# The router's scores in a cross-attention and mixture-of-experts kernel: weights stationary, four token tiles in four column groups, and a turn back

## The chip, the cores and the metric

The kernel runs on one core of one Trainium2 chip. A core has engines that work side by side, each through its own list of instructions in order: TensorE (PE in the profile; PEld is its loading of the stationary operand), VectorE (DVE), ScalarE (ACT), GpSimd (POOL) and SyncE (SP, which here only issues DMAs). The metric is the device time of one execution in microseconds; lower is better. Before the change the median of three runs is 830.52 us (829.87 to 831.75).

## The reference

One transformer layer with 4 x 1024 = 4096 tokens of width 256, all in fp32:

```python
x = x + xattn(_layernorm(x), ctx, ctx, Wq, ..., gamma, beta)   # 16 heads, 77 context rows
x = x + ffn(_layernorm(x), Wg, W1, W2, W3, Ws1, Ws2, Ws3)
# in ffn
scores = jax.nn.softmax(xf @ Wg, axis=-1)          # Wg is 256 x 32: 32 experts
weights, indices = jax.lax.top_k(scores, TOP_K)    # TOP_K = 4
# each expert e: swiglu of the tokens that chose it, times their weight, added to y
z = swiglu(xf, Ws1, Ws2, Ws3)                      # shared expert
return (y + z).reshape(B, S, D)
```

The change touches the one product `xf @ Wg`, the router's scores: 4096 tokens x 256 by 256 x 32.

## The kernel before

The 4096 tokens are 8 blocks of 512, and a block is 4 tiles of 128 (`NB`, `NC`). After a preparation stage that folds the projections of keys and values into two products per batch (`headed`, `products`; lines 237 and 262), one loop runs over the 32 tiles t. At each t it does the attention of tile t (`scores` in three groups of heads, `soften`, `divide`), turns and multiplies the probabilities of tile t-1 (`turn_p`, `output`, `residual`), and does a piece of the work for three blocks at different stages: the block ahead is normalised and turned, the block behind (`ffn`) is settled, and the block two behind (`old`) goes through the router. Everything in the loop stands in `as_written()`, which ties each engine to the order in which the code issues its instructions. So the code's order is the order on every engine.

The router of block `old` is spread over a block's four tiles: with c = t mod 4, c = 0 turns the normalised block (`turn_ffn`, result `xnT`, features on partitions), c = 1 computes the scores (`gate`), shifts them by their maximum and takes the exponential (`chances`) and picks the four best (`choose`), c = 2 marks them (`mark`), c = 3 counts and places them (`count`, `place`), and POOL then scatters the rows into DRAM (`send`, line 672). Blocks 0 to 5 go through `gate` inside the loop, at t = 9, 13, 17, 21, 25 and 29. Block y = 6 has it after the loop, and block z = 7 in the stage behind that, where the tables for the experts are made (`tables`) and the shared expert runs for y and z (`shared_in`, `shared_mid`, `shared_out`). Then come 160 expert tiles (lines 1059 to 1093) and the final gather.

`gate` makes one PSUM bank `lg` per block: for each tile c and each half k of the features, a 128 x 128 piece of `xnT` is the stationary operand and 32 columns of `wg` stream past it, so that tokens come out on partitions and experts on columns:

```python
nc.tensor.matmul(lg[:, c * NE : (c + 1) * NE],
                 xnT[:, k, c * P : (c + 1) * P], wg[:, k, :], start=(k == 0), stop=(k == KC - 1))
```

Each fp32 matmul of the code appears as two LDWEIGHTS and two MATMUL instructions in the profile; a transpose appears as one of each. DVE then reads `lg` twice (maximum at line 574, difference at line 576), and ACT takes the exponential (line 577). PSUM has 8 banks, handed out in turn by `bank`.

Of the kernel before, what the change touches and what calls it, by code (L numbers as in the profile page):

```python
# [9 lines left out]
F32 = mybir.dt.float32  # L10
I32 = mybir.dt.int32
U32 = mybir.dt.uint32
AF = mybir.ActivationFunctionType
# [3 lines left out]
P = 128  # L17
NE = 32
# [12 lines left out]
def kernel(  # L31
# [23 lines left out]
    nc = tc.nc  # L55
# [5 lines left out]
    KC = D // P  # L61
    TB = 512
    NB = T // TB
    NC = TB // P
# [22 lines left out]
    def bank(name):  # L87
        return ps.tile([P, 512], F32, tag="bank", name=name)


    ident = const.tile([P, P], F32, name="ident")
# [56 lines left out]
    sm = ctx.enter_context(tc.tile_pool(name="sm", bufs=4, side="right"))  # L148
# [5 lines left out]
    wg = late.tile([P, KC, NE], F32, name="wg")  # L154
# [255 lines left out]
    def bias_in(blk):  # L410
        nc.gpsimd.memset(qTs[blk][0:1, 0, :], 1.0)  # L411

    def scores(t, g):

        b, blk, o = t * P // (T // B), t // NC, t % NC * P
        h0, h1 = GROUPS[g]
        if g == 0:
            p = wkp.tile([P, NH, SK], F32, tag="p", name=f"p_{t}")
            su = sm.tile([P, NH], F32, tag="su", name=f"su_{t}", bufs=2)
            mx = sm.tile([P, NH], F32, tag="mx", name=f"mx_{t}", bufs=2)  # L420
            probs[t], sums[t] = p, (su, mx)
        su, mx = sums[t]
        sc = bank(f"sc_{t}_{g}")
        for k in range(KC):
            nc.tensor.matmul(  # L425
                sc[:, : (h1 - h0) * SK],
                qTs[blk][:, k, o : o + P],
                mq[:, b, k, h0 * SK : h1 * SK],
                start=(k == 0),
                stop=(k == KC - 1),  # L430
            )
        sv = sc[:, : (h1 - h0) * SK].rearrange("p (h s) -> p h s", s=SK)
        nc.vector.tensor_reduce(mx[:, h0:h1], sv, AX.X, ALU.max, negate=True)  # L433
        return sv

    def soften(t, g, sv):

        h0, h1 = GROUPS[g]
        su, mx = sums[t]
        for h in range(h0, h1):  # L440
            nc.scalar.activation(  # L441
                probs[t][:, h, :],
                sv[:, h - h0, :],
                AF.Exp,
                bias=mx[:, h : h + 1],
                accum_out=su[:, h : h + 1],
            )
# [105 lines left out]
        xnTs[blk] = xnT  # L553

    def gate(blk):
        xnT = xnTs.pop(blk)
        lg = bank(f"lg_{blk}")
        for c in range(NC):
            for k in range(KC):
                nc.tensor.matmul(  # L560
                    lg[:, c * NE : (c + 1) * NE],
                    xnT[:, k, c * P : (c + 1) * P],
                    wg[:, k, :],
                    start=(k == 0),
                    stop=(k == KC - 1),
                )
        lgs[blk] = lg

    def chances(blk):

        lg = lgs.pop(blk)
        lv = lg[:, : NC * NE].rearrange("p (c e) -> p c e", e=NE)
        mx = sm.tile([P, NC], F32, tag="rmx", name=f"rmx_{blk}", bufs=2)
        nc.vector.tensor_reduce(mx, lv, AX.X, ALU.max)
        pr = sm.tile([P, NC, NE], F32, tag="pr", name=f"pr_{blk}", bufs=2)
        nc.vector.tensor_tensor(pr, lv, mx.unsqueeze(2).to_broadcast([P, NC, NE]), ALU.subtract)
        nc.scalar.activation(pr, pr, AF.Exp)
        lgs[blk] = pr

    def choose(blk):  # L580

# [169 lines left out]
    with as_written():  # L751
        for t in range(NT):
            blk, c = t // NC, t % NC
            ffn, old = blk - 1, blk - 2
            ahead = blk + 1 < NB
            if c == 0 and blk + 2 < NB:
                xts[blk + 2] = load(blk + 2)
            if t == 0:

                nc.sync.dma_start(xr[NE * PLACES :, :], none)  # L760
                nc.sync.dma_start(
                    xr[: NE * PLACES, :].rearrange("(e q) r -> q e r", q=PLACES)[:P],
                    none.unsqueeze(1).to_broadcast([P, NE, ROW]),
                )
            if t == 18:
                nc.sync.dma_start(ws13[:, :, 0, :], Ws1.rearrange("(k p) f -> p k f", p=P))
                nc.sync.dma_start(ws13[:, :, 1, :], Ws3.rearrange("(k p) f -> p k f", p=P))
                nc.sync.dma_start(ws2, Ws2.rearrange("(k p) f -> p k f", p=P))
            if t in parts:
                load_experts(*parts[t])  # L770
            if c == 1 and ahead:
                scale_in(blk + 1)
            if c == 1 and ffn >= 0:
                measure_out(ffn, 2, 4)
            if c == 3 and ahead:
                bias_in(blk + 1)
            if c == 3:
                measure_out(blk, 0, 2)
            if c == 3 and ffn >= 0:
                measure_ffn(ffn)  # L780
            if c == 1 and old >= 0:
                gate(old)
                chances(old)
            if c == 3 and old >= 0:
                count(old)
            sv = [scores(t, g) for g in range(2)]
            soften(t, 0, sv[0])
            soften(t, 1, sv[1])
            sv.append(scores(t, 2))
            if t >= 1:  # L790
                for i in range(3):
                    turn_p(t - 1, i)
            soften(t, 2, sv[2])
            if c == 0 and old >= 0:
                turn_ffn(old)
            if c == 2 and ahead:
                turn_in(blk + 1)
            if c == 0 and ahead:
                measure_in(blk + 1)
            if c == 1 and old >= 0:  # L800
                choose(old)
            if c == 2 and old >= 0:
                mark(old)
            if c == 3 and old >= 0:
                place(old)
            invert(t)
            divide(t)
            if c == 1 and ahead:
                norm_in(blk + 1)
            if c == 3 and ffn >= 0:  # L810
                norm_ffn(ffn)
            if c == 3:
                settle(blk, 0)
            elif ffn >= 0:
                settle(ffn, c + 1)
            if c >= 2 and ahead:
                keep(blk + 1, 2 * c - 4, 2 * c - 2)
            if t >= 11:
                b11, c11 = divmod(t - 11, NC)
                send(b11, c11 * TOPK, (c11 + 1) * TOPK)  # L820
            if t >= 1:
                residual(t - 1, output(t - 1))


        z, y = NB - 1, NB - 2
        assert BA == y
        msum_a = sm.tile([P, NE], F32, tag="msum_a", name="msum_a", bufs=1)
        nc.vector.tensor_copy(msum_a, msum)
        left = [(y - 1, i) for i in range(NK)]

        def sends(n):
            for blk, i in left[:n]:
                send(blk, i, i + 1)
            del left[:n]

        del left[:4]
        measure_out(z, 2, 3)
        settle(z, 1)
        sends(3)
        turn_ffn(y)  # L840
        for i in range(3):
            turn_p(NT - 1, i)
        settle(z, 2)
        residual(NT - 1, output(NT - 1))
        measure_out(z, 3, 4)
        gate(y)
        chances(y)
        settle(z, 3)
        sends(2)
        measure_ffn(z)  # L850
# [85 lines left out]
    with as_written():  # L936
        for part in range(5):
            load_experts(*parts[NT + 1 + part])
        ta = tables("a", msum_a, NA)
        choose(y)  # L940
        shared_in(y, 0, AF.Tanh)
        norm_ffn(z)
        mark(y)
        sends(7)
        shared_mid(y, 0)
        next(ta)
        shared_in(y, 1, AF.Tanh)
        turn_ffn(z)
        count(y)
        gate(z)  # L950
        next(ta)
        place(y)
        assert not left
        left += [(y, i) for i in range(NK)]
        chances(z)
        next(ta)
        shared_mid(y, 1)
        shared_out(y)
        next(ta)
        choose(z)  # L960
        shared_in(z, 0, AF.Silu)
        mark(z)
        count(z)
        msum_z = sm.tile([P, NE], F32, tag="msum_z", name="msum_z", bufs=1)
        nc.vector.tensor_copy(msum_z, msum)
        tz = tables("z", msum_z, NJ - NA)
        sends(5)
        shared_mid(z, 0)
        place(z)
        left += [(z, i) for i in range(NK)]  # L970
        shared_in(z, 1, AF.Silu)
        shared_add(y)
        shared_mid(z, 1)
        sends(11)
        shared_out(z)
        shared_add(z)
# [261 lines left out]
```

## Time and profile before

| What | Value |
|---|---|
| Median of the timed runs | 830.52 us |
| The profiled execution: its own time | 791.69 us |
| Its span, first to last instruction | 789.9 us |
| Granted TensorE clock over the span | 0.989 |
| POOL busy | 442.3 us (56%) |
| ACT busy | 338.9 us (43%) |
| `gate` on PE (line 560) | 128 MATMULs, 14.9 us busy |
| Share of the chain that ended last: PE | 70% |
| Share of that chain: DVE, ACT, DMA, POOL | 11%, 6%, 6%, 4% |

The profiled execution is 39 us shorter than the median of the timed runs. Stages and waits are read from the profiled one; times of the two kinds are not mixed.

In the profile a line such as `L560 PE MATMUL lg<-wg,xnT 128*128 128x32` reads: line 560, TensorE, matmul that writes `lg` from `wg` and `xnT`; 128*128 is the part of the array in use (rows by columns), and 128x32 the streamed operand. The chain of waits is followed back from the last instruction, at each step to what released it. A matmul's duration includes its way through the array; what the next one has to wait for is the distance from start to start, which is shorter.

### The profile page before, as it was taken

Reading aid. Unit: us, or ns where it says so; the run is one execution under the profiler, and the core shown is the slowest. Engines: PE = TensorE matmul, PEld = TensorE weight load, DVE = VectorE, ACT = ScalarE, POOL = GpSimd, SP = SyncE. Lnnn points to the kernel's source line nnn. Section 1 sums busy time; section 2 is a strip of 40 time slices with the busy share of each in tenths; the row PEclk is TensorE's granted clock in tenths of the full one; section 3 lists DMA queues with packets and bytes.
Section 4 is the critical chain, followed back from the end, with each engine's and each line's share of the span. In section 5 each row is a group of like instructions: output and inputs, shape, how many; then the busy total and the mean of one; then the engine's idle time right before and its main releaser. Section 6 shows DMA issues by size and latency. Waiting matters only on the chain.

```text
span 789.9 us, 13517 instructions
## 1 busy us (share of the span) xinstructions
PE 756.0 (96%) x3690; PEld 574.9 (73%) x3690; DVE 546.1 (69%) x1499; ACT 338.9 (43%) x1610; POOL 442.3 (56%) x520
## 2 busy tenths in 40 slices
PE   6999999999999999999997899999999999999996
PEld 4775777777777777777774578888888888885544
DVE  1774465777777767775766676666777777775995
ACT  0647666666776567666542122222222222221110
POOL 2003333445778777677687667776555655553441
PEclk9899999999999999999998999999999999999998
DMA  9930000302317131513127646675646464626993
GB/s 288 331 93 1 1 0 2 109 25 73 107 58 236 51 116 58 163 57 110 52 94 228 198 145 195 214 228 196 184 150 187 145 193 139 195 87 245 386 404 141
DMA packets 81928, 116.21 MB, mean 147 GB/s; under 512 B 10507, under 2 KB 66239, under 8 KB 81855
## 3 DMA queue, kind: packets, MB, share of 16 engines
q1 hardware_dynamic: 61823, 68.37, 27.9%
q0 software_dynamic: 13824, 38.82, 13.5%
q10 hardware_dynamic: 6208, 8.17, 2.9%
q8 instruction: 31, 0.51, 0.3%
q14 instruction: 42, 0.34, 0.2%
HBM read 64.59 MB, written 50.73 MB: 146 GB/s over the span
## 4 chain that ended last, share of the span: by engine, by line
PE 70%; DVE 11%; ACT 6%; DMA 6%; POOL 4%; issue 3%; ACTq 0%; DVEq 0%; POOLq 0%; SPq 0%
PE peh L1067 17%; PE po L492 14%; PE sc L425 12%; PE py L1088 8%; ACT p L441 5%; PE pgT L1059 4%; DMA gy<-ys 3%; POOL xr L672 2%; PE phT L1081 2%; PE pz L728 2%; PE pvo L262 2%; PE pp L474 2%; DVE y L1146 1%; DVE mx L433 1%; PE lg L560 1%
## 5 line engine op out<-in xcount | busy, mean ns | idle before, releaser
L1093 POOL DMA_INDIRECT ys<-y,place x160 | 153.5, 959 | 90.3 <-DVE y L1092 52.0
L441 ACT ACTIVATE p<-sc,mx 128x77 f32<-128x77 f32 x512 | 159.0, 351 | 90.1 <-DVE mx L433 90.1
L1067 PE MATMUL peh<-we,gT 128*128 x640 | 164.8, 380 | 2.0 <-DVE gT L1061 1.3
L492 PE MATMUL po<-we,pT 128*128 128x256 f32 (+1 forms) x640 | 146.3, 383 | 4.6 <-DVE pT L479 4.3
L456 POOL TENSOR_TENSOR p<-p,su 128x385 f32<-128x385 f32 (+1 forms) x96 | 90.9, 972 | 105.2 <-DVE su L451 77.4
L672 POOL DMA_INDIRECT xr<-xn,row x128 | 127.8, 998 | 35.6 <-issue 33.7
L425 PE MATMUL sc<-we,qT 128*128 128x385 f32 (+1 forms) x384 | 138.1, 509 | 0.9 <-POOL qT L411 0.9
L492 PEld LDWEIGHTS po<-we,pT 128*128 128x128 f32 (+1 forms) x640 | 118.4, 190 | 25.9 <-DVE pT L479 7.9
L1075 ACT ACTIVATE h<-peh 128x128 f32<-128x128 f32 x160 | 44.3, 277 | 199.6 <-PE peh L1067 199.6
L441 ACT ACTIVATION_READ_ACCUMULATOR p<-sc,mx 128x1 f32 x512 | 119.2, 233 | 0.0
L1067 PEld LDWEIGHTS peh<-we,gT 128*128 128x128 f32 x640 | 109.2, 190 | 10.7 <-DVE gT L1061 1.5
L425 PEld LDWEIGHTS sc<-we,qT 128*128 128x128 f32 x384 | 71.6, 189 | 53.6 <-issue 25.4
L1076 DVE TENSOR_TENSOR h<-peh,h 128x128 f32<-128x128 f32 x160 | 46.5, 291 | 74.4 <-ACT h L1075 73.2
L1088 PE MATMUL py<-we,ehT 128*128 x320 | 95.6, 381 | 0.0
L433 DVE TENSOR_REDUCE mx<-sc 128x5 f32<-128x385 f32 (+1 forms) x96 | 54.7, 580 | 44.0 <-PE sc L425 43.7
L1092 DVE TENSOR_SCALAR y<-py,own 128x256 f32<-128x256 f32 x160 | 77.4, 484 | 0.9 <-PE py L1088 0.6
L1061 DVE COPY gT<-pgT 128x256 f32<-128x256 f32 x160 | 66.3, 414 | 0.0
L1059 PE MATMUL pgT<-ident,g 128*128 128x128 f32 x320 | 61.1, 273 | 0.0
L1088 PEld LDWEIGHTS py<-we,ehT 128*128 128x128 f32 x320 | 48.3, 191 | 12.2 <-ACT ehT L1083 0.3
L1059 PEld LDWEIGHTS pgT<-ident,g 128*128 128x128 f32 x320 | 44.7, 141 | 16.0 <-PE phT L1081 0.3
L728 PE MATMUL pz<-ws,hT 128*128 128x256 f32 x128 | 34.3, 419 | 11.7 <-DVE hT L717 6.9
L474 PEld LDWEIGHTS pp<-ident,p 128*128 128x128 f32 x320 | 36.1, 139 | 11.4 <-issue 5.5
(200 smaller groups left out, 997.3 us busy)
## 6 DMA issues: line engine op xcount, KB each, us to landing
g<-xr SPq DMA_DIRECT2D x160, 136.0 KB, 3.1
gy<-ys SPq DMA_DIRECT2D x16, 1024.0 KB, 7.9
xr<-y SPq DMA_DIRECT2D x1, 4352.0 KB
y<-in_x SPq DMA_DIRECT2D x8, 512.0 KB, 5.1
out<-y ACTq DMA_DIRECT2D x16, 256.0 KB, 5.4
xnd<-xnT SPq DMA_DIRECT2D x6, 512.0 KB
we<-in_W SPq DMA_DIRECT2D x8, 384.0 KB, 5.3
ys<-y,place POOLq DMA_INDIRECT x160, 2.5
```

The lines of the kernel that those rows point to most:

```text
L425: nc.tensor.matmul(sc[:, : (h1 - h0) * SK], qTs[blk][:, k, o : o + P], mq[:, b, k, h0 * SK : h1 * SK], start=(k == 0), stop=(k == KC - 1),)
L433: nc.vector.tensor_reduce(mx[:, h0:h1], sv, AX.X, ALU.max, negate=True)
L441: nc.scalar.activation(probs[t][:, h, :], sv[:, h - h0, :], AF.Exp, bias=mx[:, h : h + 1], accum_out=su[:, h : h + 1],)
L456: nc.gpsimd.tensor_tensor(p[:, h0:h1, :], p[:, h0:h1, :], su[:, h0:h1].unsqueeze(2).to_broadcast([P, h1 - h0, SK]), ALU.mult,)
L492: nc.tensor.matmul(po[:, :D], pT[:n, i, :], vo[b][:n, i, :], start=(i == 0), stop=(i == KT - 1))
L672: sct = nc.gpsimd.indirect_dma_start(out=xr, out_offset=bass.IndirectOffsetOnAxis(ap=row[:, i : i + 1], axis=0), in_=xn[:, c, :], in_offse ...
L1059: nc.tensor.transpose(pt[:, k * P : (k + 1) * P], g[:, j % RG, k * P : (k + 1) * P], ident)
L1061: nc.vector.tensor_copy(gT.rearrange("p k t -> p (k t)"), pt[:, :D])
L1067: nc.tensor.matmul(ph[:, : 2 * H], gT[:, k, :], we[:, ds(ev[j] * EW + k * 2 * H, 2 * H)], start=(k == 0), stop=(k == KC - 1),)
L1088: nc.tensor.matmul(py[:, :D], hT, we[:, ds(ev[j] * EW + KC * 2 * H, D)], start=True, stop=True)
L1092: nc.vector.tensor_scalar(y, py[:, :D], own[:, i, 1:2], None, ALU.mult)
L1093: sent = nc.gpsimd.indirect_dma_start(out=ys, out_offset=bass.IndirectOffsetOnAxis(ap=place_[:, i : i + 1], axis=0), in_=y, in_offset=None,)
```

## The change

`gate` swaps the operands. The weights `wg[:, k, :]`, 128 x 32, are stationary, and a 128 x 128 piece of `xnT` streams. The result of tile c has experts on partitions and tokens on columns, and lands on partitions 32c to 32c + 31 of the bank; `tile_position=(0, c * NE)` places it in columns 32c to 32c + 31 of the array. The loop order is turned: k outside, c inside. So `lg[:, :128]` holds four groups of 32 experts below one another.

A new `turn_gate` brings it back: ACT copies `lg[:, :128]` into the tile `pr`, TensorE transposes it as one 128 x 128 piece into a new bank `lt`. `chances` reads `lt` in place of `lg`, and its exponential is moved into a function of its own, `powers`. In the loop `gate` stays ahead of the first two `scores`; `turn_gate` and `chances` come behind them, and `powers` comes behind the first `soften`. In the two later places `turn_gate` stands just ahead of `chances` and `powers` just behind it.

```diff
     def gate(blk):
         xnT = xnTs.pop(blk)
         lg = bank(f"lg_{blk}")
-        for c in range(NC):
-            for k in range(KC):
+        for k in range(KC):
+            for c in range(NC):
                 nc.tensor.matmul(
-                    lg[:, c * NE : (c + 1) * NE],
+                    lg[c * NE : (c + 1) * NE, :P],
+                    wg[:, k, :],
                     xnT[:, k, c * P : (c + 1) * P],
-                    wg[:, k, :],
                     start=(k == 0),
                     stop=(k == KC - 1),
+                    tile_position=(0, c * NE),
                 )
         lgs[blk] = lg
+    def turn_gate(blk):
+        pr = sm.tile([P, NC, NE], F32, tag="pr", name=f"pr_{blk}", bufs=2)
+        flat = pr.rearrange("p c e -> p (c e)")
+        nc.scalar.copy(flat, lgs.pop(blk)[:, :P])
+        lt = bank(f"lt_{blk}")
+        nc.tensor.transpose(lt[:, :P], flat, ident)
+        lgs[blk] = lt, pr
     def chances(blk):
-        lg = lgs.pop(blk)
-        lv = lg[:, : NC * NE].rearrange("p (c e) -> p c e", e=NE)
+        lt, pr = lgs.pop(blk)
+        lv = lt[:, : NC * NE].rearrange("p (c e) -> p c e", e=NE)
...
-        pr = sm.tile([P, NC, NE], F32, tag="pr", name=f"pr_{blk}", bufs=2)
         nc.vector.tensor_tensor(pr, lv, mx.unsqueeze(2).to_broadcast([P, NC, NE]), ALU.subtract)
-        nc.scalar.activation(pr, pr, AF.Exp)
         lgs[blk] = pr
+    def powers(blk):
+        nc.scalar.activation(lgs[blk], lgs[blk], AF.Exp)
...
             if c == 1 and old >= 0:
                 gate(old)
-                chances(old)
             if c == 3 and old >= 0:
                 count(old)
             sv = [scores(t, g) for g in range(2)]
+            if c == 1 and old >= 0:
+                turn_gate(old)
+                chances(old)
             soften(t, 0, sv[0])
+            if c == 1 and old >= 0:
+                powers(old)
             soften(t, 1, sv[1])
...
         gate(y)
+        turn_gate(y)
         chances(y)
+        powers(y)
...
+        turn_gate(z)
         chances(z)
+        powers(z)
```

## The prediction

> **What bounds the kernel now.** I read the table of stretches first, for the stages in which the router runs. Its columns are the stretch, its length, then PE, PEld, DVE, ACT and POOL busy, clock, DMA share and GB/s.
>
> ```profile
> 150.00:380.00 230.00, 228.27 (x1107) 173.67 (x1107) 170.28 (x463) 153.22 (x802) 160.07 (x198) 1.00 0.32 101
> 400.00:430.00 30.00, 23.17 (x120) 16.27 (x118) 21.16 (x74) 10.14 (x20) 24.25 (x30) 0.95 0.58 181
> 450.00:700.00 250.00, 248.31 (x1372) 208.71 (x1373) 176.93 (x585) 65.75 (x303) 160.62 (x168) 1.00 0.55 177
> ```
>
> In the loop (150 to 380 us) PE is busy 99% of the time; every other engine has a quarter or more to spare. Between loop and experts (400 to 430) it is not: PE idles 7 of 30 us. The experts are again 99% PE. So time saved on PE in the loop should reach the end, and time saved between the stages only where PE or its successor ends the wait.
>
> Next the chain of waits around one gate (start, duration, what), here t = 13:
>
> ```profile
> 189.59 4.32 PE po L492 x20
> 193.92 1.71 PE lg L560 x16
> 195.62 4.23 PE sc L425 x12
> ```
>
> PE goes from `output` through the gate into `scores` without a gap: the gate is 1.71 us of PE, 16 steps of 107 ns, though only 32 columns stream in each. The rows of the tile `lg` say what paces it: loads of 128 columns at 192 ns each, overlapping their neighbours.
>
> ```profile
> L560 PEld LDWEIGHTS lg<-wg,xnT x128: 188/192/192, 149.8 to 424.0; 128*128 128x128 f32 x128
> L560 PE MATMUL lg<-wg,xnT x128: 193/276/277, 150.0 to 424.0; 128*128 128x32 f32 x128
> ```
>
> **The new gate on PE.** It removes 16 wide loads with 32-column streams and adds 16 narrow loads (32 columns) with 128-column streams. One such stream costs 109 ns: `turn_ffn`'s transposes (line 547) are 8 of 128 columns in 0.87 us. One after the other, 16 would take 1.74 us, as much as now. All depends on whether the four column groups run side by side. No row has column groups, but the preparation has row groups: `products` alternates between two halves of 64 rows. The chain shows it beside `headed`, same 308 columns, whole array:
>
> ```profile
> 43.44 8.30 PE pkT L237 x32
> 51.74 8.49 PE pm L262 x64
> ```
>
> `headed` takes 259 ns an instruction, `products` 133 ns: the two row groups overlap fully, and this with fp32 and its two instructions to a matmul. If column groups do as well, the 16 fall into 4 rounds of 4: 4 x 0.109 + 0.02 for starting offsets = 0.46 us. I take this value, as the nearest row. The bounds are 0.46 (all four overlap), 0.98 (only neighbours overlap: 9 steps of 0.109) and 1.74 (none).
>
> **The change of array shape.** The Trainium skill speaks against the change here: "TensorEngine Tiling (Array Packing)", Key Properties, says that changing the tiling mode drains TensorE. The trace has such a change in the table step, which uses a 32 x 32 corner between whole-array matmuls:
>
> ```profile
> 424.04 0.28 PE L560 MATMUL lg<-wg,xnT 128*128 128x32 f32 x1
> 424.25 0.22 PE L891 MATMUL p_end_a<-nt_a,tri_in 32*32 32x1 f32 x2
> 424.39 0.70 PE L728 MATMUL pz<-ws,hT 128*128 128x256 f32 x2
> ```
>
> The last `lg` would hand over at 424.04 + 0.11 = 424.15; `p_end` starts at 424.25, so going in costs 0.10. It then takes 0.14 for two one-column matmuls of some 0.05 each: 0.04 on the way out. And the first two `pz` end after 0.70, where the usual step of 0.216 (`po`: 4.32 / 20) plus 0.38 gives 0.60: another 0.10 for a load that is no longer hidden. Together 0.25 us per round trip. Were the drain free, each gate would gain 0.25 more.
>
> The same skill, "TensorE: Matmul & The Clock Gate", Part 3, What overlaps and what doesn't, says that a load overlaps running matmuls only where the row group differs, and that matmuls run strictly in order. Column groups share all their rows, so by the rule the loads would lie bare: a quarter of the 107 ns of a wide one, 27 ns each (an estimate), 0.43 us per gate, and strict order with two instructions to a matmul would allow neighbours alone to overlap. By the rule the gate is 0.98 + 0.43 = 1.41 us, by the rows 0.46. The `lg` rows contradict the first half: loads of 192 ns start every 107 ns on the same 128 rows, beside matmuls of 276 ns. The `pm` row contradicts the second: neighbours alone would also give 133 ns there, but the trace starts two of them together at the very first (eight instructions span 1.31 us from 51.67 on: 0.10 for a bare load, 3 more pair steps of 0.26 and a 0.42 end, so the pairs fill from the start). I follow the rows.
>
> **The turn back on PE.** One transpose, 0.11 us (0.87 / 8). In the loop it stands behind the first two `scores`, 2.9 us after the gate; the copy that it needs is done long before.
>
> Sum per gate in the loop: 0.10 + 0.46 + 0.15 + 0.11 = 0.82 against 1.71, a gain of 0.89 us. Six such gates: **5.3 us**.
>
> **ACT and DVE in the loop.** ACT gets a copy of 128 x 128 (0.31 us, as the exponential of the same shape). It falls into time in which ACT waits anyway:
>
> ```profile
> L577 ACT ACTIVATE pr<-pr 128x128 f32<-128x128 f32 x8 | 2.5, 309 | 30.5 <-DVE pr L576 30.5
> ```
>
> Eight exponentials had 30.5 us of idle time before them, 2.94 at t = 13. The exponential itself moves out of that idle time into the softmax stream, where 11 heads of 0.30 follow. It delays ACT by 0.31, and by nothing for its input: `pr` should be ready about 0.1 us before `soften` 0 ends (the second maximum ends 0.85 after its scores, then two DVE steps of 0.3). Behind it queue `soften` 1, ACT's copies of `pT`, and for those PE waits in `output`. At t = 13 ACT's copy ends at 201.98 and the ninth `po`, its first reader, starts at 202.92: 0.94 us of cover. Without it each gate would pay 0.3. On DVE the two small steps (0.26 and 0.29) move behind two maxima, into the 0.73 us for which DVE waits for the third group of scores. The extra bank per gate shifts the rotation by one; each bank it meets had its last reader over 1 us earlier. POOL's `divide` of t-1 ends at 196.0, PE's `turn_p` starts at 199.7 and would at 198.8: still covered. I cost these at nothing.
>
> **Block y, after the loop.** Here `turn_gate` follows at once, so PE waits for the copy: gate 410.08 to 410.64 (0.10 + 0.46), 0.17 until the result is out, copy 0.31 plus handover 0.09, bare load 0.10, transpose 0.11: the shared expert starts at 411.4 where it started at 411.79. That gains nothing, because PE then waits for ACT's normalised block:
>
> ```profile
> 419.74 0.33 PE L547 MATMUL pxn<-ident,xn 128*128 128x128 f32 x1 [0.16 <-ACT xn L362]
> 420.24 0.33 PE L547 MATMUL pxn<-ident,xn 128*128 128x128 f32 x1 [0.16 <-ACT xn L362]
> 420.73 0.44 PE L547 MATMUL pxn<-ident,xn 128*128 128x128 f32 x2 [0.16 <-ACT xn L362]
> ```
>
> These waits come from POOL's sends and its pow (line 347), which the gate does not touch. They also swallow a late start: with no overlap the shared expert would start 0.9 late, and the fourth transpose still come on time. Zero.
>
> **Block z.** PE goes from the gate (422.45) to `p_end`, and DVE waits for it:
>
> ```profile
> 424.50 0.15 DVE L893 COPY end_a<-p_end_a 32x1 f32<-32x1 f32 x1 [1.46 <-PE p_end_a L891]
> 429.86 0.80 PE L728 MATMUL pz<-ws,hT 128*128 128x256 f32 x1 [4.76 <-DVE hT L720]
> ```
>
> From there DVE is busy without a gap until `hT` at 429.8, for which PE waits 4.76 us. So `p_end` decides. It comes 1.80 after the gate's start; it will come 0.10 + 0.46 + 0.10 = 0.66 after it, 1.14 us earlier, less than DVE's idle 1.46. POOL's sends end that wait nowhere. Copy and transpose fall into PE's idle 4.76. Gain **1.1 us**; what is late next is DVE's own chain, unchanged.
>
> **Sum:** 5.3 + 1.1 = 6.4 us off the profiled 791.69. The runs shown have a median 39 us above that execution; I take the gain over in microseconds (stretched alike it would be 6.7): 830.52 - 6.4 = **824.1 us**.
>
> **The rivals.**
>
> *Only neighbours overlap* (0.98 per gate): gains 0.37 x 6 + 0.6 = 2.8 us, **827.7**. For it: that rule of strict order; against it: the first pair of `pm`.
>
> *Column groups take turns, slower than before.* The place is line 560. Row groups read different rows, while four column groups each stream all 128 rows of different data; no row shows that this can be fed side by side. Against it: the same Part 3 gives a measured 2.38 times for three column tiles, from which I estimate 1.74 x 3 / (4 x 2.38) = 0.55 for the gate, near my 0.46; no row here shows it. Price per gate: 0.10 + 1.74 + 0.15 + 0.11 = 2.10, a loss of 0.39, six times 2.4, and 0.1 at block z: **833.0**. It decides from the point at which 16 streams take over 1.35 us (1.71 less 0.36), 84 ns a step. With bare loads in addition (0.43 x 7) it would be 836.
>
> *The PE gain is eaten by ACT* since copy and exponential cost 0.62 per gate: only where the cover of 0.94 is gone. All six would then lose up to 0.3 each: 825.9, inside the range.
>
> **How the numbers follow.** Full overlap 0.54, neighbours 0.21, taking turns 0.20, other losses 0.05. Likeliest: 824.1, by itself 822.5 to 826.5. The range 822.5 to 833.0 takes in the neighbours and most of turn-taking. A difference of 0.2% (1.7 us) is about what a measurement of this kernel can tell from none. Faster by more: all of the first, nearly all of the second: 0.72. Slower by more: most of the third, part of the others: 0.18. Within: 0.10.
>
> **What would show it.** In the changed profile: line 560's loads with 128*32 and its starts in groups of four; chain pieces from `po` to `sc` of 0.7 us instead of 1.71; `lt` without a wait in the loop; `pT` ready before the ninth `po`; PE's wait for `hT` unchanged at block z. Wrong if those starts stand 0.1 us apart, or if the first `sc` behind a gate starts over 1.3 us after the gate.

## The result, and the profile after

| | Median | Lowest to highest | Runs |
|---|---|---|---|
| Kernel before | 831.01 us | 829.87 to 831.75 us | 4 |
| Changed kernel | 825.71 us | 824.51 to 826.42 us | 4 |

The ratio is 0.9934, with a 95% interval of 0.9918 to 0.995. By the medians it is 5.3 us faster, by the interval 4.2 to 6.8, where 6.4 had been forecast.

One thing has to be known before the profiles are compared. The kernel before takes about 790 us on some chips and about 830 us on others: 789.87, 789.95 and 790.81 us beside three groups of the experiments below, 831.01 and 830.33 us beside the first comparison and one later run. By its length, its profile came from a chip of the first kind, the changed kernel's from one of the second. So the two are compared only in the loop and in the stage just behind it. For what comes later, a profile of the changed kernel from a chip of the first kind (e5_after_again) is used.

The gate on the chain of waits of the changed kernel, at the same t = 13 as in the prediction (start us, us, what):

```profile
188.67 4.34 PE po L492 x20
193.01 0.57 PE lg L561 x16
193.59 3.04 PE sc L425 x8
196.63 0.11 PE lt L576
196.74 1.29 PE sc L425 x4
```

The gate was 1.71 us and is 0.57 (with the way in), and 0.11 for the transpose. From the gate's start to the end of the `scores` it is 5.01 where it was 5.94. The `scores` in it (3.04 + 1.29 against 4.23) are hardly dearer than before: by the single starts they take 4.24, where they took 4.22. The first `scores` matmul behind the new gate keeps PE for 0.49 instead of the usual 0.39, because its load lies bare, but behind the old gate it already took 0.47.

The rows of the tile `lg` in the changed kernel (nanoseconds, minimum/median/maximum):

```profile
L561 PEld LDWEIGHTS lg<-xnT,wg x128: 106/110/110, 150.1 to 417.7; 128*32 128x32 f32 x128
L561 PE MATMUL lg<-xnT,wg x128: 272/273/297, 150.1 to 417.8; 128*32 128x128 f32 x128
```

These are the same 16 loads and 16 streams per gate as before. Sixteen loads of some 108 ns would be 1.73 us, if each waited for the end of the one before; the whole gate is 0.57.

How they lie is seen in the timeline of the changed kernel around that gate (start us, busy us, instruction, and in brackets the idle time before it and what ended that):

```profile
192.94 0.38 PEld L561 LDWEIGHTS lg<-xnT,wg 128*32 128x32 f32 x16 [0.33 <-ACT xnT L548]
192.94 0.65 PE L561 MATMUL lg<-xnT,wg 128*32 128x128 f32 x16
...
193.51 3.11 PE L425 MATMUL sc<-we,qT 128*128 128x462 f32 x8
...
193.65 0.27 ACT L574 COPY pr<-lg 128x128 f32<-128x128 f32 x1 [0.78 <-PE lg L561]
...
197.14 0.28 DVE L584 TENSOR_REDUCE rmx<-lt 128x4 f32<-128x128 f32 x1
...
197.92 0.33 ACT L589 ACTIVATE pr<-pr 128x128 f32<-128x128 f32 x1
```

All 16 loads are done in 0.38 us: they lie on one another. In the single starts of these matmuls, four stand 7 ns apart (192.941, .948, .954, .961), and the next fours follow 0.11 to 0.13 later (193.074, 193.184, 193.293). That is the picture of four column groups side by side, in four rounds. (The records do not name the column group; that a four holds one stream of each is read from the starts.) Before the first there is a gap of 0.09 (the last `po` would hand over at 192.85), behind the last stream one of 0.09, then the bare load. ACT's copy falls into idle time of ACT, and the exponential stands behind the first softmax group without a wait.

The table of stretches of the changed kernel, for the loop and the experts (stretch, length, PE, PEld, DVE, ACT and POOL busy, clock, DMA share, GB/s):

```profile
150.00:380.00 230.00, 228.27 (x1134) 168.65 (x1134) 173.97 (x472) 156.86 (x824) 164.29 (x203) 1.00 0.32 102
450.00:700.00 250.00, 226.37 (x1186) 183.41 (x1187) 155.02 (x511) 58.13 (x261) 138.25 (x144) 0.97 0.49 155
```

The same table of the changed kernel on a chip of the first kind:

```profile
450.00:700.00 250.00, 248.71 (x1377) 209.35 (x1376) 177.83 (x584) 66.18 (x304) 160.73 (x168) 1.00 0.55 176
```

The loop is as full of PE as before, so what PE gained, the loop gained. In the expert stage the first profile shows 22 us of idle PE that the second does not. It looks as if the change had cost something there, but the changed kernel on a chip of the first kind does not show it, and the timed gain is the same on both: as far as these profiles show, it goes with the kind of chip. The same holds for a wait at block z that the first profile shows and several expectations below ask about:

```profile
421.10 0.15 DVE L910 COPY end_a<-p_end_a 32x1 f32<-32x1 f32 x1 [3.15 <-remote]
```

DVE stands for 3.15 us there, and for 3.08 in e9_powers_first, the other profile from a chip of the second kind. In both profiles of the changed kernel from chips of the first kind it is 0.33. What ends the long wait is not shown.

### The profile page after: what moved, and what is told of

It reads as the page before. It is cut to its first block, busy times and chain, and to the rows that moved or that the text cites. A ratio compares the mean times of both kernels' runs of the same rounds, so it can differ in the third digit from the quotient of the medians.

```text
span 823.8 us, 13559 instructions
## 1 busy us (share of the span) xinstructions
PE 760.3 (92%) x3698; PEld 566.7 (69%) x3698; DVE 546.1 (66%) x1499; ACT 342.4 (42%) x1618; POOL 441.7 (54%) x520
## 4 chain that ended last, share of the span: by engine, by line
PE 68%; DVE 11%; ACT 6%; DMA 5%; issue 5%; POOL 4%; another core or an unknown queue 1%; ACTq 0%; DVEq 0%; POOLq 0%; SPq 0%
PE peh L1086 17%; PE po L492 12%; PE sc L425 11%; PE py L1107 8%; ACT p L441 5%; PE pgT L1078 4%; DMA gy<-ys 3%; PE pp L474 3%; PE phT L1100 2%; PE pz L739 2%; POOL xr L683 2%; PE pvo L262 2%; DVE y L1165 1%; PE pvo L287 1%; DVE gy L1164 1%
## 5 line engine op out<-in xcount | busy, mean ns | idle before, releaser
L1086 PE MATMUL peh<-we,gT 128*128 x640 | 169.4, 388 | 17.4 <-issue 11.6
L1086 PEld LDWEIGHTS peh<-we,gT 128*128 128x128 f32 x640 | 111.1, 194 | 29.5 <-issue 13.3
L1107 PE MATMUL py<-we,ehT 128*128 x320 | 97.4, 387 | 1.5 <-ACT ehT L1102 0.8
L1100 PE MATMUL phT<-ident,h 128*128 128x128 f32 x160 | 44.4, 278 | 8.5 <-DVE h L1095 5.8
L1102 ACT COPY ehT<-phT 128x128 f32<-128x128 f32 x160 | 41.7, 260 | 9.3 <-PE phT L1100 4.6
```

Of the source, the lines that this page charges most:

```text
L1086: nc.tensor.matmul(ph[:, : 2 * H], gT[:, k, :], we[:, ds(ev[j] * EW + k * 2 * H, 2 * H)], start=(k == 0), stop=(k == KC - 1),)
L1100: nc.tensor.transpose(pt[:, :P], h, ident)
L1107: nc.tensor.matmul(py[:, :D], hT, we[:, ds(ev[j] * EW + KC * 2 * H, D)], start=True, stop=True)
```

## The experiments

The marks used below are read from each trace: the loop from the first `scores` of t = 0 to the last `scores`; block y from the last `output` to POOL's last pow (line 347); block z from that pow to the `pz` that waits for `hT`.

**The kernel before, twice more.** No edit; a measure of what repeats.

> The kernel before, unchanged, profiled on the same chip as the other runs. Its profile of before is 39 us shorter than its timed runs, and the profile of the changed kernel is as long as its timed runs, so the two can't be compared stage by stage behind 450 us. If the 39 us lie in the expert stage for every kernel on this chip, the span here is about 828 us and the stretch from the first expert to the last is some 35 us longer than in the earlier profile. If the earlier profile was only an odd execution in the loop too, the loop differs as well. The ratio to itself should be 1.000 within 0.002.

> The kernel before once more, together with the changed one. Two kinds of executions have been seen: near 790 us and near 830 us, both for the kernel before. If this pair runs near 830, its profile of before should show the same idle stretches in the expert stage as the profile after (PE waits of 0.4 to 8 us at peh and phT behind 446 us), and a wait of ScalarE or VectorE for about 3 us behind p_end if that belongs to the place and not to the change. Near 790 it should show neither.

Ratios 1.000 (0.9989 to 1.001) and 1.001 (1.0 to 1.002). The loop took 333.30 and 333.51 us, block y 7.45 in both, block z 12.54 in both. These stages repeat to 0.2 us or better. What lies behind them does not: from that `pz` to the first expert matmul it was 20.62 and 20.04.

**The changed kernel, twice more**, on the same chips as other experiments.

> The changed kernel, on the chip of the other experiments, whose kernel before takes 790 us. The sum of the parts there: the loop alone gave 0.9931, the tail alone 0.9994. If the parts add, the ratio is 0.9925, 5.9 us; if the wait of ScalarE and VectorE for 3 us at block z belongs to the change, it shows again and the ratio stays at 0.9934; if it belonged to that execution, the wait at block z is 0.3 us.

> The changed kernel beside it. By the parts measured (loop 5.4, block y -0.2, block z 1.0) 6.2 us below before, ratio 0.992; by the two ratios so far (0.9934 and 0.9936) 5.2 us.

Ratios 0.9936 (0.9917 to 0.9956) and 0.9937 (0.9915 to 0.9958): 784.77 against 789.95 us and 785.52 against 790.81. The loop took 327.88 and 328.07, block y 7.67 in both, block z 11.56 and 11.55.

**The new gate in the loop alone.** Blocks 0 to 5 go through the new `gate`, y and z through the old one (the old functions kept as `gate_old` and `chances_old`).

```diff
-        gate(y)
-        turn_gate(y)
-        chances(y)
-        powers(y)
+        gate_old(y)
+        chances_old(y)
...
-        gate(z)
+        gate_old(z)
...
-        turn_gate(z)
-        chances(z)
-        powers(z)
+        chances_old(z)
```

> The new gate for blocks 0 to 5 in the loop, the old one for y and z. If all that is gained comes from PE in the loop (0.89 us for each of six gates), the time is that of the changed kernel, 5.3 us below before, ratio 0.9936. If block z pays its 1.1 us, this run is 1.1 us behind the changed kernel. If the tail costs something (the 3 us wait of ScalarE and VectorE at block z in the profile after), this run is faster than the changed kernel.

Ratio 0.9931 (0.9914 to 0.9948), 784.93 against 789.87 us. The loop took 328.03, that is 5.3 less than before; blocks y and z took 7.47 and 12.54, as before. All that the timed runs can tell of the change is in the loop.

**The new gate behind the loop alone.** The converse.

```diff
             if c == 1 and old >= 0:
-                gate(old)
+                gate_old(old)
+                chances_old(old)
...
-            if c == 1 and old >= 0:
-                turn_gate(old)
-                chances(old)
...
-            if c == 1 and old >= 0:
-                powers(old)
```

> The old gate in the loop, the new one for y and z. By the prediction block y gives 0 and block z 1.1 us: ratio 0.9987. If the wait at block z belongs to the change, this run is 1 to 2 us slower than before, ratio 1.001 to 1.002. If the tail doesn't matter at all, 1.000.

Ratio 0.9994 (0.9978 to 1.0009), 789.51 us: the timed runs cannot tell it from none. The marks can. The loop is as before (333.30), block z is 1.0 shorter (11.54), and block y, which should have kept its length, is 0.22 **longer** (7.67).

For block z, the timeline of this run:

```profile
422.57 0.22 PE L929 MATMUL p_end_a<-nt_a,tri_in 32*32 32x1 f32 x2
...
422.83 0.15 DVE L931 COPY end_a<-p_end_a 32x1 f32<-32x1 f32 x1 [0.33 <-PE p_end_a L929]
...
428.31 1.22 PE L764 MATMUL pz<-ws,hT 128*128 128x256 f32 x2 [4.52 <-DVE hT L756]
```

DVE's wait for `p_end` was 1.46 and is 0.33, 1.13 less, and PE's wait for `hT` is still there, so what DVE gains reaches the end. Some 0.13 of it is lost again in DVE's own steps between `end_a` and `hT`: 5.48 where it was 5.35.

For block y, POOL's sends and DVE's settling step. First the timeline of the kernel before (e1_before_again):

```profile
412.42 0.96 POOL L672 DMA_INDIRECT xr<-xn,row  x1 [0.30 <-issue]
412.65 0.47 DVE L518 SCALAR_TENSOR_TENSOR qb<-qb,mv,gamma_b 128x256 f32<-128x256 f32 x1
413.40 0.24 POOL L507 TENSOR_SCALAR ve<-mv 128x1 f32<-128x1 f32 x1
```

And the new gate behind the loop alone:

```profile
411.41 0.48 DVE L518 SCALAR_TENSOR_TENSOR qb<-qb,mv,gamma_b 128x256 f32<-128x256 f32 x1
411.53 1.19 POOL L708 DMA_INDIRECT xr<-xn,row  x1 [0.30 <-issue]
412.74 0.24 POOL L507 TENSOR_SCALAR ve<-mv 128x1 f32<-128x1 f32 x1
```

The quicker router lets DVE reach its settling step (line 518, two inputs from SBUF) earlier: 0.12 us **before** POOL's third send starts, where it used to start 0.23 behind that start. The send then takes 1.19 instead of 0.96, and since POOL's chain of sends and pow ends block y, 0.23 goes straight onto the path. Other sends in the same stretch that start inside such a DVE step are long too: in the kernel before, 409.55 us, 0.32 of the step left, send 1.30; 414.49, 0.33 left, send 1.29. The Trainium skill, "SBUF — State Buffer", Who interferes with whom, says that a DVE instruction with two SBUF inputs contends with a GpSimd instruction that reads SBUF, and that the order of issue decides who blocks. The order of starts above agrees with it. No run moved the settling step on purpose, but in two of the runs below it falls elsewhere. In "Tile outside" it starts 0.07 before the send, not 0.12:

```profile
407.31 0.52 DVE L518 SCALAR_TENSOR_TENSOR qb<-qb,mv,gamma_b 128x256 f32<-128x256 f32 x1
407.38 0.96 POOL L683 DMA_INDIRECT xr<-xn,row  x1 [0.30 <-issue]
```

There the send keeps its 0.96, the step itself grows from 0.48 to 0.52, and block y takes 7.44, as before the change. In the swap without column groups the step comes 1.45 us behind that send's start and the send takes 0.96 too; the send after it takes 1.09 instead of 1.29, and block y 7.25. So the loss of 0.22 does hang on where this step falls, and some 0.05 us decide it; it is no fixed price of the change. By the starts alone the page's rule would have delayed the send in "Tile outside" as well; why a lead of 0.07 did not and one of 0.12 did stays open.

**Turning at once.** `turn_gate` directly behind `gate` in the loop, as in block y.

```diff
                 gate(old)
+                turn_gate(old)
...
-                turn_gate(old)
                 chances(old)
```

> As the changed kernel, but in the loop the copy and the transpose stand right behind the gate, ahead of the scores, so PE waits for ScalarE's copy. At block y of the profile after, where they stand so, PE needs 1.19 us from the first gate matmul to the next stage against 0.85 in the loop with the transpose counted in. Expected: 0.35 us more for each of six gates, 2.1 us slower than the changed kernel, ratio to before 0.996. A rival: other engines hide it and the time is that of the changed kernel.

Ratio 0.9958 (0.9943 to 0.9974), 787.41 us; loop 330.32, so 2.44 more than the changed kernel's, 0.41 per gate. The chain of waits of this run shows what the changed kernel hides:

```profile
193.37 0.62 PE lg L561 x16
193.99 0.02 issue
194.01 0.27 ACT pr L574
194.28 0.04 issue
194.33 0.33 PE lt L576
194.66 4.15 PE sc L425 x12
```

PE stands for the copy and the handovers; with the first two `scores` in between, it is never seen. Somewhat under half of the gate's gain hangs on this one place in the order.

**Tile outside, half inside.** The order of the eight matmuls as it was before the change, to see whether it matters that neighbours in the program lie in different column groups.

```diff
-        for k in range(KC):
-            for c in range(NC):
+        for c in range(NC):
+            for k in range(KC):
```

> The changed kernel with the loops of the gate in the old order: c outside, k inside. Each column group then gets its two matmuls, four streams, in a row. If TensorE holds a queue for each column group, the four groups still fill at once and nothing changes: gate 0.57 us on the chain, ratio that of the changed kernel. If it starts matmuls strictly in the order of the code, only the last stream of one group overlaps the first of the next: 13 steps of 0.109, 1.4 us, the gate 0.85 us longer, six times, 5.1 us, so the time is about that of before.

Ratio 0.9933 (0.9915 to 0.9951), 784.86 against 784.77 us for the changed kernel on the same chip; loop 327.99 against 327.88. The gate on the chain of waits of this run:

```profile
193.43 0.59 PE lg L561 x16
```

It is 0.59 instead of 0.57, where strict order would have made it some 1.4 us. The single starts stand 13 ns apart here (193.357, .370, .384, .397) but still four together. So the order of these matmuls in the code does not decide how they overlap.

**The same swap without column groups.** The weights stationary, all 512 tokens of a half in one stream, four small transposes back; `lgT` is the tile for ACT's copy.

```diff
-            for c in range(NC):
-                nc.tensor.matmul(
-                    lg[c * NE : (c + 1) * NE, :P], wg[:, k, :], xnT[:, k, c * P : (c + 1) * P],
...
+            nc.tensor.matmul(lg[:NE, :], wg[:, k, :], xnT[:, k, :], start=(k == 0), stop=(k == KC - 1))
...
-        nc.tensor.transpose(lt[:, :P], flat, ident)
+        for c in range(NC):
+            nc.tensor.transpose(lt[:, c * NE : (c + 1) * NE], lgT[:, c * P : (c + 1) * P], ident[:NE, :NE])
```

> The operands swapped but without column groups: wg stays in 32 columns, all 512 tokens of a block stream past it in two matmuls of 512, and four transposes of 32 x 128 turn the result back. Only the overlap is taken away. Four streams of 512 columns[...] are 1.71, as much as the old gate; with 0.25 for the change of shape, and four transposes with a second change of shape, about 0.6, the gate costs 2.5 against 1.71 before: 0.8 slower in the loop for each of six, 5 us, ratio 1.006. If swapping alone brought the gain, the ratio would be below 1.

Ratio 1.0084 (1.0063 to 1.0104), 797.49 us: slower than the kernel before. Loop 338.12, 0.80 per gate more. The chain of waits of this run:

```profile
149.48 1.83 PE lg L560 x4
151.31 3.04 PE sc L425 x8
154.35 0.36 PE lt L569 x4
154.71 1.50 PE sc L425 x4
```

The same columns stream one after the other in 1.83 us where four groups take 0.57, and the transposes and their surroundings come on top: 6.73 in all, against 5.94 before. The four streams start 0.43 apart. The swap by itself is a loss; the gain is the column groups. The loop accounts for 4.8 of the 7.5 us; block z is 1.2 longer (13.76), block y 0.2 shorter, and the marks do not place the rest.

**The exponential first.** `powers` ahead of the first `soften`, on a chip of the second kind.

```diff
-            soften(t, 0, sv[0])
-            if c == 1 and old >= 0:
                 powers(old)
+            soften(t, 0, sv[0])
```

> The changed kernel with the exponential of the scores in front of the first soften in the loop, not behind it. ScalarE works in order, so it then waits for VectorE's difference: in the profile after, at t = 13, that ends at 197.82 while soften 0 starts at 196.10. The softmax stream starts 1.7 us later and the copies of pT with it, 1.7 + 0.3 less the 0.3 it has now. Their cover is 0.85 in the profile after. If that cover is what hides ScalarE, PE waits about 0.9 us more in output at each of six gates, 5 us in all, and the time is about that of before. If ScalarE is not near PE's path at all, the time is that of the changed kernel, ratio 0.9935.

Ratio 1.0039 (1.0019 to 1.006), 834.03 against 830.33 us: **slower than the kernel before**. Loop 335.74 where the changed kernel on such a chip has 328.05, 1.28 per gate; 0.9 had been expected. The chain of waits of this run, behind the gate:

```profile
197.94 0.30 DVE pr L585
198.24 0.02 issue
198.26 0.02 ACTq L589
198.28 0.04 issue
198.32 0.31 ACT pr L589
198.63 3.37 ACT p L441 x22
202.00 0.48 ACT pT L479
202.49 0.04 issue
202.53 2.64 PE po L492 x11
```

The whole softmax of 11 heads queues on ACT behind one small exponential, which waits for DVE, which waits for the transpose. ACT begins 2.2 us later (198.32 against 196.10), its copy of `pT` comes late, and the ninth `po` waits for it. It comes 2.84 behind the first, where it comes 1.83 in the changed kernel, and then its own load of 0.10 lies bare as well: 1.11 in all, more than the 0.9 expected. About 0.2 more per block comes at the next c = 0, where the ninth `po` has hardly any cover even in the changed kernel (0.16). The move of `powers` is not decoration: with it in the wrong place, the change loses.

**Counting in two matmuls.** A version to go further with: the changed kernel, with `count` cut down in the same spirit. The counts of the tiles ahead are summed on DVE, and one matmul with ones replaces four.

```diff
-        tot = sm.tile([P, NE], F32, tag="tot", name=f"tot_{blk}", bufs=2)
-        nc.vector.tensor_reduce(tot, mask.rearrange("p c e -> p e c"), AX.X, ALU.add)
-        nc.vector.tensor_tensor(tot, tot, msum, ALU.add)
+        for c in range(1, NC):
+            nc.vector.tensor_tensor(pre[:, c, :], pre[:, c - 1, :], mask[:, c - 1, :], ALU.add)
...
-        for d in range(1, NC):
-            nc.tensor.matmul(pf[:, d * NE : NC * NE], ones,
-                mask[:, : NC - d, :].rearrange("p c e -> p (c e)"), start=False, stop=False)
...
+        nc.tensor.matmul(pf[:, : NC * NE], ones, ahead.rearrange("p c e -> p (c e)"), start=False, stop=True)
```

> The changed kernel, and the same reading applied to count: its ten steps are paced by loads of 128 columns while 32 to 128 stream. VectorE adds up the masks ahead (four additions of 128 x 32 in place of a reduction and an addition, about 0.2 us more), and count becomes two matmuls, four steps in place of ten. PE saves 6 x 0.107 = 0.64 for each of six blocks in the loop, 3.9 us, and 0.3 to 0.6 in the tail, where VectorE gives back 0.2. Expected about 4.3 us below the changed kernel, ratio to before 0.987. A rival: VectorE's 0.2 us at c = 2 delays the maxima behind it and PE waits; then the gain is under 2 us.

Ratio to the kernel before 0.9892 (0.9874 to 0.991), 781.82 us, against 784.77 for the changed kernel on the same chip: the fastest of all. The count on the chain of waits, in the changed kernel (e5_after_again):

```profile
171.80 0.22 PE pf L634 x2
172.03 0.59 PE pf L636 x6
172.62 0.30 PE pf L643 x2
```

And with two matmuls:

```profile
171.22 0.22 PE pf L637 x2
171.44 0.22 PE pf L638 x2
```

That is 0.67 less per block; the loop gave 3.20 in six, 0.53 each, where 0.64 had been expected. About half of the missing 0.8 is the ninth `po` at c = 0: in the changed kernel it starts 0.16 behind ACT's copy of `pT` (at t = 20, 0.05), here 0.05 every time, which is the handover, and 0.03 to 0.13 later after the first. Block z gave nothing (11.54). With the cover at c = 0 used up, a further cut of PE in the loop would run into ACT there.

## Why the prediction was right

By its steps, with the marks of e1_before_again against e5_after_again:

| Step | Forecast | Measured |
|---|---|---|
| Full overlap of four column groups | 0.46 us | 0.48, first start to the end of the last stream |
| Way in | 0.10 | 0.09 |
| Way out | 0.04 and a load of 0.10 | 0.09 and a load of 0.11 (0.08 of it already behind the old gate) |
| Transpose in the loop, without a wait | 0.11 | 0.11 |
| Six gates in the loop | -5.3 | -5.42 (0.90 each) |
| ACT's 0.31 more, against a cover of 0.94 for the ninth `po` at t = 13 | 0 | 0, cover 0.85 |
| Block y | 0 | **+0.22** |
| Block z | -1.1 | -0.98 |
| Sum up to the shared expert of z | -6.4 | -6.2 |
| Timed | -6.4 | -5.3 (4.2 to 6.8) |

- **The loop** was right in mechanism and size. The row groups of the preparation were the right row to read column groups from, and the quoted rule, from which 1.41 us had been worked out, was not what the chip did: measured is 0.48. That the size fits to 0.01 us is in part luck. The way out was 0.05 dearer than forecast and the streams 0.02, while the bare load, booked as a new cost of 0.10, cost only 0.02 more than behind the old gate; the errors cancel. The old gate's steps were also read a little short: 107 ns is the mean with a first step of 30 ns, the others start 112 ns apart. The sum uses the 1.71 in one piece and does not suffer from it.
- **Block y** was wrong. The step that failed is "these waits come from POOL's sends and its pow, which the gate does not touch". The gate does not touch POOL, but it moves DVE's settling step 0.35 us ahead against POOL's send, and with the step there the send is longer. It cost 0.22.
- **Block z** was right in mechanism; `p_end` came 1.13 earlier against its input, 1.14 had been worked out. Of this 0.15 went again into DVE's steps behind it, which the prediction had called unchanged.
- **The timed gain** is smaller than the sum of the marks: 5.3, 5.2 and 5.3 us on the three occasions, against 6.2. All three intervals reach 6.2, and the stretch from `pz` to the first expert matmul differs from one profile of the same kernel to the next: 20.04 to 20.62 before, 20.24 and 21.26 changed. Whether a microsecond is given back there stays open. The loop alone and the tail alone were timed at 4.9 and 0.4.
- **The rivals.** Neighbours alone and groups taking turns fall by the starts in fours. ACT eating the gain did not happen, but the exponential put first shows that its mechanism is real, with over 1 us per gate.

## What to carry to other kernels

Where few columns stream past wide stationary tiles, swapping the operands paid here only together with column groups: four groups took 0.57 us where the same streams one after the other took 1.83. Put the way back (a copy and a transpose) behind other work of PE, and a small activation behind the stream that the next matmuls wait for: the two places were worth 0.41 and 1.28 us per gate here, against a gain of 0.90. When a stage is ended by an engine that the change does not touch, look also at what the change moves **beside** it: a DVE step shifted by 0.35 us made a POOL send 0.23 longer, and with a shift 0.05 smaller it did not.

## What the runs showed of the hardware

- Four column groups of 32 columns, fp32, ran side by side at no visible loss: 16 loads of 108 ns were over in 0.38 us and 16 streams in 0.48, though all four groups read the same 128 rows. The Trainium skill, "TensorE: Matmul & The Clock Gate", Part 3, What overlaps and what doesn't, has loads overlap only across row groups, and starts in strict order. Neither held here: 16 loads on the same rows overlapped the streams, and with the four matmul instructions of one group next to each other in the program, four streams still started within 40 ns.
- A round trip between the whole array and 32-column groups cost 0.09 in, 0.09 out and a bare load of 0.11: 0.29 us, of which the old gate, without a change of shape, had 0.08 as well.
- That POOL's sends grew by 0.23 to 0.34 us when they started 0.12 to 0.16 us after the start of a DVE step with two SBUF inputs had not been reckoned with; in the trace of before it was there to be read (sends of 960 ns and of 1.3 us in the same stretch).
- The same kernel takes 790 us on some chips and 830 on others. In the two profiles from chips of the second kind, PE has issue gaps in the expert stage that none of the others has. From the page of the changed kernel:

```profile
L1086 PE MATMUL peh<-we,gT 128*128 x640 | 169.4, 388 | 17.4 <-issue 11.6
```

and from the page of the same kernel on a chip of the first kind:

```profile
L1086 PE MATMUL peh<-we,gT 128*128 x640 | 164.8, 380 | 2.0 <-DVE gT L1080 1.3
```

Before its matmuls PE idles 17.4 us against 2.0. No profile of the kernel before on a chip of the second kind exists, and the cause of these gaps stays open; the ratio of the change was the same on both kinds.
